# Key gathers and softmax steps of the last four groups of a two-layer graph attention network, done in layer 1's sums' stage instead of its table stage

## The chip, the cores and the metric

The kernel runs on one core of one Trainium2 chip. The metric is the device time of one launch in microseconds. The core has five engines that work side by side, each in the order of its own instructions: PE (TensorE: products and transposes, which write to PSUM), DVE (VectorE), ACT (ScalarE), POOL (GpSimd, which here issues the indirect DMAs, the gathers) and SP (SyncE, which issues most other DMAs).

## What is computed

A graph of 3125 nodes with 53125 edges, sorted by their target `dst`, runs through two layers of relational attention with 3 relations, first with 4 heads and then with 1. The result is added to the input and normalized per row.

```
def rgat_conv(x, W, q, k, b, src, dst, etype, heads, out_ch, n_nodes):
    xr = jnp.einsum('nd,rdf->rnf', x, W)
    oi = xr[etype, dst]
    oj = xr[etype, src]
    qi = oi @ q
    kj = oj @ k
    alpha = jax.nn.leaky_relu(qi + kj, NEG_SLOPE)
    m = jax.ops.segment_max(alpha, dst, num_segments=n_nodes)
    e = jnp.exp(alpha - m[dst])
    z = jax.ops.segment_sum(e, dst, num_segments=n_nodes)
    a = e / (z[dst] + EPS)
    msg = (a[:, :, None] * oj.reshape(-1, heads, out_ch)).reshape(-1, heads * out_ch)
    out = jax.ops.segment_sum(msg, dst, num_segments=n_nodes)
    return out + b

h = elu(rgat_conv(x, W1, q1, k1, b1, ..., 4, 192, n))
out = layernorm(x + rgat_conv(h, W2, q2, k2, b2, ..., 1, 768, n))
```

## The kernel before

Nodes stand in 25 blocks of up to 128 rows. Edges, too, are handled in 25 groups: group b holds the edges of the targets of one block, in 17 slots of 128 edges (14 in group 0), so 14 + 24 x 17 = 422 slots in all. One gather reads, for one slot, one row for each of its 128 edges.

After a preparation (edges in order, per-node scores, weights split into a high and a low part) there are three stages.

**The table stage (`phase1`)** multiplies the blocks 1 to 24 with `W1` for each relation and half: 24 x 6 = 144 products groups (`d_group`, L698, 18 matmuls each), whose results ACT copies (`d_row`, L713) and SP stores in the table `ftab1` (L715). In the same stage the softmax of every edge group of layer 1 is worked out. Its code is a loop over a tick `n`: in each tick the events listed for it come first, and then one products group. For edge group b the events are, with the tick relative to 6b:

- `a_loads`, `a_loads2` (-10, -9): SP loads of the group's edges. `a_index`, `a_index2`, `a_next`, `a_next2` (-6 to -4): a transpose on PE (L541), the indices on DVE, and the start of the next group, each a short exchange of PE and DVE.
- `a_gathers` (-5): the 17 key gathers on POOL (L462, tile `kt`, from the table `kt1` of 4 scores per row), into one of three key buffers.
- `a_q`, `a_q2`, `a_q3` (1 to 3): DVE compares the edges with the node numbers (L601, L603), PE picks each edge's query score (17 small matmuls, L613), DVE reduces them to `qe` (L625, L629).
- `a_window` (2): an SP load of the masks for the scan.
- `a_alpha` (4): DVE adds keys and queries (L634, L636); it needs all keys of the group. `a_max` (5): three transposes on PE (L642). `a_scan` (6): a scan forward and one back on DVE (L650, L651), a subtraction (L654) and the exponential on ACT (L655). `a_back` (7): a transpose back on PE (L659). `a_put` (8): a copy to `pall` (L662), where the weights of all groups are kept. Groups below 8 do these five two ticks later.

Each products group also waits, at three of its matmuls, for a key gather of the edge group that stands at the same place in the order:

```
if n % 6 == 0:
    tc.add_manual_dep(m.ins, gathered[g, (3 * k + n // 6) * slots(g) // 18].name, behind,
                      reason="an even load")
```

In the last 24 ticks ACT also loads layer 2's split weights into the places of `W1` that are free (`second_weights`, L514).

**Layer 1's sums' stage (`phase2`)** is a loop over `k`, one slot each. POOL gathers the slot's rows of `ftab1` (L462, tiles `share` and `g`, 14 buffers in turn); two steps later than it could read them, DVE writes the slot's selection masks times the softmax weights (`high`, L854), and PE sums the rows by target (`sums`, L876) in two batches per group, after 9 and after 17 slots. Each group's sums then go through `e_y` to `e_s2` (DVE, ACT and a transpose on PE, L928) and are multiplied with `W2` (`d_part`, L953, spread over the next group's slots), copied by ACT (L961) and stored by SP in the table of layer 2 (L967). POOL's queue holds the key gathers of the stage before ahead of the first row gather; the last third of the weights of `W2` is loaded by ACT behind the first group's exponential.

**Layer 2's sums' stage (`phase3`)** gathers rows of layer 2's table (tile `G`), works out layer 2's softmax and sums (L1147), and normalizes and stores the result.

The order in each stage is written by hand (the dictionary `ev` of ticks); the compiler does not reorder it. PSUM and SBUF buffers are taken in turn from pools, so a writer waits for the last reader of its buffer.

Of the kernel before, what the change touches and what calls it, by code (L numbers as in the profile page):

```python
# [8 lines left out]
F32 = mybir.dt.float32  # L9
# [4 lines left out]
AF = mybir.ActivationFunctionType  # L14
ALU = mybir.AluOpType
# [5 lines left out]
P = 128  # L21
NEG_SLOPE = 0.2
# [15 lines left out]
SL = 17  # L38
# [10 lines left out]
ROUNDS = ((0, 7, 15), (1, 8, 16), (2, 9, 14), (3, 11), (4, 12), (5, 13), (6, 10))  # L49

BATCHES = ((0, 1, 2), (3, 4, 5, 6))


@with_exitstack
def kernel(
# [19 lines left out]
    nc = tc.nc  # L75
    N, D = x.shape
    R = layers[0]["W"].shape[0]
    E = src.shape[0]
    NB = (N + P - 1) // P
# [4 lines left out]
    H1 = l1["H"]  # L84
# [9 lines left out]
    V, S, G, T = nc.vector, nc.scalar, nc.gpsimd, nc.tensor  # L94
# [6 lines left out]
    ed_d = dram.tile([4, LL], F32, name="ed_d")  # L101
# [3 lines left out]
    kt1 = dram.tile([NP * R, 4], F32, name="kt1")  # L105
# [4 lines left out]
    ident = keep.tile([P, P], F32, name="fident")  # L110
    make_identity(nc, ident)
    row = keep.tile([P, P], F32, name="frow")
# [22 lines left out]
    dl = keep.tile([P, NB, SL + 1], F32, name="fdl")  # L135
    rel = keep.tile([P, NB, SL], F32, name="rel")
    pall = keep.tile([P, NB, SL, H1], F32, name="pall")
# [303 lines left out]
    def base(b):  # L441

        return SLF + (b - 1) * SL if b else 0

    def slots(b):
        return SL if b else SLF

    def slot(k):

        return divmod(k - SLF + SL, SL) if k >= SLF else (0, k)  # L450
# [4 lines left out]
    regs = {}  # L455

    def gather_rows(to, tab, b, j):

        i = ridx[:, b]
        if b in first_rows:  # L460
            i = rfirst[:, first_rows[b]]
        return G.indirect_dma_start(out=to, out_offset=None, in_=tab, in_offset=_index(i[:, j:j + 1]),  # L462
                                    bounds_check=NP * R - 1, oob_is_err=False)

    def start(b, into):

        if b == 0:
            return 0
        if b not in into:
            into[b] = nc.sync.value_load(starts[0:1, 0, b:b + 1], min_val=0, max_val=E)  # L470
        return into[b]
# [7 lines left out]
    def at(t, rw, off, ap, s):  # L479

        c = t[rw:rw + 1, bass.ds(s + (FRONT + off), 1)]
        return bass.AP(tensor=c.tensor, offset=c.offset, ap=ap)
# [37 lines left out]
    def phase1(pre, work, psum, wH, wL, qq):  # L520
# [96 lines left out]
        def a_q3(b):  # L617
            s = st[b]
            pq = s["pq"]
            nq = H1 * R * 3  # L620
            hs = (SL + 1) // 2
            tq = work.tile([P, SL, H1, R * 3], F32, name="tq", bufs=1)
            for c in range(2):
                n = min(hs, SL - c * hs)
                V.tensor_tensor(tq[:, c * hs:c * hs + n],  # L625
                                pq[:, c, :n * nq].rearrange("p (j h k) -> p j h k", j=n, h=H1),
                                s["oh"][:, c * hs:c * hs + n, None, :].to_broadcast([P, n, H1, R * 3]), op=ALU.mult)
            s["qe"] = work.tile([P, SL, H1], F32, name="qe", bufs=2)
            V.tensor_reduce(s["qe"], tq, AX.X, ALU.add)  # L629

        def a_alpha(b):
# [56 lines left out]
        def d_group(n, b, r, c):  # L688

            g, k = divmod(n, 6)  # L690
            po = psum.tile([P, 512], F32, name="po", bufs=2)
            xT = xt[b]
            n = 0
            for t in range(DT):
                i = r * DT + t
                sl = slice(c * HALF, (c + 1) * HALF)
                for s, w in ((0, wH), (0, wL), (1, wH)):
                    m = T.matmul(po[:, :HALF], xT[:, s, t, :], w[:, i, sl], start=(n == 0), stop=(n == 3 * DT - 1))  # L698
                    if n % 6 == 0:
                        tc.add_manual_dep(m.ins, gathered[g, (3 * k + n // 6) * slots(g) // 18].name, behind,  # L700
                                          reason="an even load")
                    n += 1
            st["po", b, r, c] = po

# [67 lines left out]


        GB = NB - 4
        groups = [(b, r, c) for b in range(1, GB) for r in range(R) for c in range(2)]
        groups += [(b, r, c) for r in range(R) for b in range(GB, NB) for c in range(2)]
        ev = {}

        chain = ((-6, a_index), (-6, a_index2), (-5, a_gathers), (-5, a_next), (-4, a_next2))
        for b in range(1, NB):  # L780
            for d, f in chain:
                ev.setdefault(6 * b + d + (b == 1), []).append((f, b))
        steps = ((-10, a_loads), (-9, a_loads2), (1, a_q), (2, a_q2),
                 (2, a_window), (3, a_q3), (4, a_alpha), (5, a_max), (6, a_scan), (7, a_back), (8, a_put))
        for b in reversed(range(NB)):
            for d, f in steps:

                d += 2 * (d >= 4 and b < 8) + (b == 2 and d == -10)
                if 6 * b + d >= 0:
                    ev.setdefault(6 * b + d, []).append((f, b))  # L790
        ev[6 * NB - 10].append((lambda b: a_last(), 0))
        for b in range(2, GB + 1):
            for d, f, o in ((-8, d_turn, 0), (-7, d_split, 0), (-7, x_next, 1)):
# [32 lines left out]
    def phase2(work, psum, wH, wL):  # L826
# [9 lines left out]
        st = {}  # L836
        blk = {}
        order = range(NB)

        def in_turn(k):  # L840

# [3 lines left out]
        def gather(k):  # L845
            gather_rows(gs[k % NG], tab1, *in_turn(k))

        def high(k):

            b, j = in_turn(k)  # L850
            lo, hi = WINDOW[j][0] * 32, WINDOW[j][-1] * 32 + 32
            sel = work.tile([P, H1, 64], F32, name="selp", bufs=12)
            for h in range(H1):
                V.tensor_scalar(sel[:, h, :hi - lo], row[:, lo:hi], dl[:, b, j:j + 1], pall[:, b, j, h:h + 1],  # L854
                                op0=ALU.is_equal, op1=ALU.mult)
            st[b, j] = sel, gs[k % NG]

# [116 lines left out]
        def when(k, f, *a):  # L974
            ev.setdefault(k, []).append((f, a))
# [5 lines left out]
        for i, b in enumerate(order):  # L981
            e = SLF + i * SL + LAG
            if i > 0:
                for d, f in ((0, e_y), (1, e_x), (2, e_h), (3, e_t), (4, e_s), (4, e_s2)):
                    when(e + d, f, b)
            e += 6
            for m in range(6 * R):
                rc = divmod(m // 3, 2)
                k = e + m * SL // (6 * R) if i else first + 5 + m * (SL + 3) // (6 * R)
                when(k, d_part, b, *rc, m % 3)  # L990
                if m % 3 == 2:
                    when(k + 1, d_row, b, *rc)
            when(e + 2 + SL, d_q, b)
        for k in range(max(ev) + 1):
            if k < NK:
                gather(k)
            if k in (19, 20, 23, 26, 28):
                next(last_w2, None)
            if 0 <= k - LAG < NK:
                sums(k - LAG)  # L1000
            if k == first:
                e_first(order[0])
            if 0 <= k - LAG + 2 < NK:
                high(k - LAG + 2)
            for f, a in ev.get(k, []):
                f(*a)
            if k == NK + LAG:
                for b in range(len(xbs)):
                    x_load3(b)
# [882 lines left out]
```

## Time and profile before

| what | value |
|---|---|
| time, median of 3 runs | 2060.18 us (2058.1 to 2061.2) |
| the profiled execution | 2060.05 us, span 2058.3 us |
| mean granted TensorE clock | 0.915 |
| first key gather, first products group | 120.2 us, 123.0 us |
| last key gather | 692.6 us |
| first row gather of layer 1's sums | 693.9 us |
| first row gather of layer 2's sums | 1475.5 us |
| PE busy | 1761.5 us (86%) |
| POOL busy | 1327.4 us (64%) |
| DVE busy | 1185.0 us (58%) |

Times within the execution count from the first instruction. PE's busy time is that of pipelined matmuls, so a busy PE is not PE at its peak. In a line of the timeline, the bracket at the end is the engine's idle time before that instruction and what ended it; "issue" there means that nothing the profile shows was waited for.

### The profile page before, as it was taken

The page shows a single profiled execution, that of the slowest core. Times are in us where ns is not written, and L with a number is a line of the kernel's source. Part 1 is how long each engine was busy: PE and PEld are TensorE (multiplying, and loading weights), DVE is VectorE, ACT ScalarE, POOL GpSimd, SP SyncE. Part 2 cuts the span into 40 slices and gives each one's busy share as a digit, 9 for nine tenths or more (in the row PEclk, how much of TensorE's full clock was granted, in tenths as well). Part 3 has the DMA queues.
Part 4 walks back from the last instruction along what each step waited for, and adds up shares of the span by engine and source line. Part 5 has one row for each costly group of instructions (what it writes and reads, how often), then busy time and mean ns, then how long its engine had stood idle before and what let it go on. Part 6 is the DMA issues. An engine that isn't in the chain of part 4 may idle for free.

```text
span 2058.3 us, 41812 instructions
## 1 busy us (share of the span) xinstructions
PE 1761.5 (86%) x15027; PEld 1482.8 (72%) x15027; DVE 1185.0 (58%) x4163; ACT 374.1 (18%) x659; POOL 1327.4 (64%) x1326
## 2 busy tenths in 40 slices
PE   6989998999999579999999999999666766776775
PEld 5979998899899368988898888888523433433433
DVE  6545554555454456776677667666356556556654
ACT  5421211222111011111111111111102112112111
POOL 4257777777777745556555655564277777777773
PEclk9999999999999889999999999999877777787787
DMA  7655554555547687778777877876699999999993
GB/s 194 192 140 167 176 189 139 172 160 180 176 153 233 216 311 252 258 264 286 250 264 271 279 261 257 280 267 206 223 313 329 343 339 330 339 328 320 320 328 133
DMA packets 156844, 506.31 MB, mean 246 GB/s; under 512 B 43875, under 2 KB 57069, under 8 KB 156628
## 3 DMA queue, kind: packets, MB, share of 16 engines
q0 software_dynamic: 81904, 331.52, 48.2%
q1 hardware_dynamic: 62926, 156.02, 21.8%
q10 hardware_dynamic: 11798, 16.00, 2.3%
q8 instruction: 122, 2.00, 0.4%
q14 instruction: 94, 0.77, 0.1%
HBM read 412.55 MB, written 95.69 MB: 247 GB/s over the span
## 4 chain that ended last, share of the span: by engine, by line
PE 55%; issue 15%; POOL 14%; DMA 10%; DVE 5%; ACT 1%; POOLq 0%; ACTq 0%; DVEq 0%; SPq 0%
PE po L953 23%; PE acc L876 11%; POOL kt L462 11%; PE acc L1147 10%; PE po L698 4%; DMA G<-ftab,ridx 4%; POOL G L462 3%; DMA kt<-kt,ridx 2%; DMA wL<-w_d 2%; PE bank L285 1%; PE pt L263 1%; PE po L395 1%; PE pt L928 1%; DVE F L1107 1%; PE bc L1054 1%
## 5 line engine op out<-in xcount | busy, mean ns | idle before, releaser
L953 PE MATMUL po<-wH,hT 128*128 128x386 f32 (+1 forms) x1800 | 486.7, 345 | 8.5 <-DMA wH<-w_d 5.9
L462 POOL DMA_INDIRECT kt<-kt,ridx x374 | 395.5, 1057 | 114.0 <-issue 110.9
L698 PE MATMUL po<-wH,xT 128*128 128x384 f32 x1584 | 440.6, 348 | 9.7 <-ACT share L713 4.4
L462 POOL DMA_INDIRECT G<-ftab,ridx x374 | 374.2, 1001 | 114.0 <-issue 91.2
L854 DVE TENSOR_SCALAR selp<-frow,fdl,pall 128x32 f32<-128x32 f32 (+1 forms) x1688 | 381.1, 322 | 0.0
L953 PEld LDWEIGHTS po<-wH,hT 128*128 128x128 f32 x1800 | 331.7, 190 | 24.4 <-issue 21.0
L462 POOL DMA_INDIRECT share<-ftab,ridx x239 | 238.4, 997 | 169.8 <-PE acc L876 125.6
L953 PE MATMUL po<-wL,hT 128*128 128x386 f32 (+1 forms) x900 | 306.7, 341 | 4.8 <-DMA wL<-w_d 4.8
L698 PEld LDWEIGHTS po<-wH,xT 128*128 128x128 f32 x1584 | 294.7, 192 | 15.4 <-ACT share L713 6.2
L1147 PE MATMUL acc<-G,selp 128*32 128x386 f32 x2388 | 290.0, 582 | 2.9 <-DVE selp L1133 1.5
L698 PE MATMUL po<-wL,xT 128*128 128x384 f32 x792 | 270.3, 341 | 0.0
L1147 PEld LDWEIGHTS acc<-G,selp 128*32 128x32 f32 x2388 | 178.3, 128 | 77.3 <-issue 45.9
L462 POOL DMA_INDIRECT g<-ftab,ridx x135 | 135.7, 1005 | 108.3 <-PE acc L876 83.0
L876 PE MATMUL acc<-share,selp 128*32 128x193 f32 x3208 | 185.3, 330 | 2.7 <-DMA share<-ftab,rfirst 1.3
L961 ACT COPY r<-po 128x386 f32<-128x386 f32 (+1 forms) x150 | 72.3, 482 | 592.9 <-PE po L953 581.6
L953 PEld LDWEIGHTS po<-wL,hT 128*128 128x128 f32 x900 | 171.3, 190 | 5.2 <-DMA wL<-w_d 5.2
L1060 DVE TENSOR_SCALAR sT<-bc,cols 128x512 bf16<-128x512 f32 (+1 forms) x125 | 83.4, 667 | 150.6 <-PE bc L1054 147.9
L876 PEld LDWEIGHTS acc<-share,selp 128*32 128x32 f32 x3208 | 125.7, 111 | 44.0 <-issue 7.7
L698 PEld LDWEIGHTS po<-wL,xT 128*128 128x128 f32 x792 | 151.7, 191 | 0.0
L1054 PE MATMUL bc<-d,one 1*128 1x512 bf16 (+1 forms) x125 | 48.5, 388 | 85.2 <-DVE sT L1060 82.1
L713 ACT COPY share<-po 128x384 f32<-128x384 f32 x144 | 67.8, 477 | 275.2 <-PE po L698 268.2
L876 PE MATMUL acc<-g,selp 128*32 128x193 f32 x1768 | 115.0, 328 | 1.6 <-DMA g<-ftab,rfirst 1.2
(262 smaller groups left out, 1911.5 us busy)
## 6 DMA issues: line engine op xcount, KB each, us to landing
ftab<-share SPq DMA_DIRECT2D x75, 386.0 KB
ftab<-r SPq DMA_DIRECT2D x75, 386.0 KB
share<-in_L_gnn_W_dram SPq DMA_DIRECT2D x36, 384.0 KB
w_d<-w2hl SPq DMA_DIRECT2D x18, 768.0 KB
sT<-dr_d SPq DMA_DIRECT2D x25, 544.0 KB
share<-in_x_dram SPq DMA_DIRECT2D x27, 384.0 KB
xb_d<-share SPq DMA_DIRECT2D x25, 384.0 KB
xr<-in_x_dram SPq DMA_DIRECT2D x21, 384.0 KB
```

Of the source, the lines that this page charges most:

```text
L263: T.transpose(pt[:, f, c * P:(c + 1) * P], a[:, (2 * i + f) * P:(2 * i + f + 1) * P], ident)
L285: T.matmul(to, a[:, 2 * i + f, :], t[:, f, :w], start=(n == 0), stop=(n == 2 * DT - 1))
L462: return G.indirect_dma_start(out=to, out_offset=None, in_=tab, in_offset=_index(i[:, j:j + 1]), bounds_check=NP * R - 1, oob_is_err=False)
L698: m = T.matmul(po[:, :HALF], xT[:, s, t, :], w[:, i, sl], start=(n == 0), stop=(n == 3 * DT - 1))
L713: S.copy(to, po[:, :HALF].rearrange("p (h f) -> p h f", h=2))
L854: V.tensor_scalar(sel[:, h, :hi - lo], row[:, lo:hi], dl[:, b, j:j + 1], pall[:, b, j, h:h + 1], op0=ALU.is_equal, op1=ALU.mult)
L876: T.matmul(acc[32 * t:32 * t + 32, h // 2, c], sel[:, h, 32 * (t - WINDOW[i][0]):][:, :32], g[:, h * CW:(h + 1) * CW], start=(i == u[0] an ...
L953: T.matmul(po[:, :wd], hT[:, k, t, :], w[:, r * DT + t, sl], start=(t == 0 and n == 0), stop=(t == DT - 1 and n == 2))
L961: S.copy(o[:, c * HW:c * HW + wd], po[:, :wd])
L1054: T.matmul(bc[:, :n], one, s["d"][:, 4 * i * P:4 * i * P + n], start=True, stop=True)
L1060: V.tensor_scalar(s["sT"][:, 4 * i * P:4 * i * P + n], bc[:, :n], cols[:, b:b + 1], None, op0=ALU.is_equal)
L1147: T.matmul(acc[32 * t:32 * t + 32, c, :HW], st[b, j][:, 32 * (t - WINDOW[j][0]):][:, :32], gs[:, (base(b) + j) % NG, c * HW:(c + 1) * HW], ...
```

## The change

The edge groups 21 to 24 (`LATE = 4`) no longer have their keys gathered and their softmax finished in the table stage. Their query scores (`a_q` to `a_q3`) stay there, written to `pall`, which later takes the weights in the same place. Their 68 key gathers go into the loop of layer 1's sums, four at a time (`KEYS = 4`) behind the fourteenth row gather of each of groups 2 to 18, into two new key buffers. Once a group's 17 keys are issued, its mask load, alpha, transposes, scan, exponential, transpose back and copy follow, as `l_load` to `l_put`, 5 to 11 slots behind the sums of group 8, 12, 16 and 20. They use the buffers `y`, `ey` and `pt` of that stage's other steps.

In the table stage, the gathers and softmax steps of the other 21 groups (354 slots) are spread over all 144 ticks: group b stands at tick `turn[b] = base(b) * 144 // 354`, where `base(b)` is its first slot, so one group every 6.9 ticks instead of every 6. All of them now do the last five steps two ticks later. `a_index` to `a_next2` keep their ticks of 6b. The products' waits are for the gather at the same share of 354. The selection masks of layer 1's sums get 8 narrow and 7 wide buffers instead of 12 wide ones.

```diff
+LATE = 4
+KEYS = 4
...
-            s["qe"] = work.tile([P, SL, H1], F32, name="qe", bufs=2)
+            s["qe"] = work.tile([P, SL, H1], F32, name="qe", bufs=2) if b < NB - LATE else pall[:, b]
...
-                        tc.add_manual_dep(m.ins, gathered[g, (3 * k + n // 6) * slots(g) // 18].name, behind,
-                                          reason="an even load")
+                        tc.add_manual_dep(m.ins, gathered[slot((18 * g + 3 * k + n // 6) * NE // (3 * len(groups)))].name,
+                                          behind, reason="an even load")
...
+        NE = base(NB - LATE)
...
+        turn = [base(b) * len(groups) // NE for b in range(NB - LATE)]
         for b in range(1, NB):
             for d, f in chain:
-                ev.setdefault(6 * b + d + (b == 1), []).append((f, b))
+                if f is not a_gathers:
+                    ev.setdefault(6 * b + d + (b == 1), []).append((f, b))
+                elif b < NB - LATE:
+                    ev.setdefault(max(turn[b] + d, 6 * b + d + (b == 1)), []).append((f, b))
         steps = ((-10, a_loads), (-9, a_loads2), (1, a_q), (2, a_q2),
                  (2, a_window), (3, a_q3), (4, a_alpha), (5, a_max), (6, a_scan), (7, a_back), (8, a_put))
+        taken = [n + 2 for n in turn]
+        for b in range(NB - LATE, NB):
+            n = 6 * b + 2
+            while min(abs(n - t) for t in taken) < 2:
+                n += 1
+            taken.append(n)
+            turn.append(n - 2)
         for b in reversed(range(NB)):
             for d, f in steps:
-                d += 2 * (d >= 4 and b < 8) + (b == 2 and d == -10)
-                if 6 * b + d >= 0:
-                    ev.setdefault(6 * b + d, []).append((f, b))
+                if b >= NB - LATE and (d >= 4 or f is a_window):
+                    continue
+                if d == -10:
+                    n = 6 * b + d + (b == 2)
+                elif d == -9:
+                    n = turn[b] - (9 if b < 12 else 4)
+                else:
+                    n = turn[b] + d + 2 * (d >= 4)
+                if n >= 0:
+                    ev.setdefault(n, []).append((f, b))
...
+        kts = [work.tile([P, SL, H1], F32, name=f"kt{i}", bufs=1) for i in range(2)]
+        al = work.tile([P, SL + 2, H1], F32, name="al", bufs=1)
...
+        keys = [(b, j) for b in range(NB - LATE, NB) for j in range(SL)]
+        late = {}
+        def key(b, j):
+            gather_rows(kts[b % 2][:, j, :], kt1, b, j)
+        def l_load(b):
+            t = work.tile([P, D], F32, name="y", bufs=1)[:H1 * SL]
+            late["f"], late["e"] = t[:, :3 * P + 1], t[:, 3 * P + 1:4 * P + 1]
+            nc.sync.dma_start(late["f"], at(ed_d, 3, -P - 1, [[P, SL], [0, H1], [1, 3 * P + 1]], start(b, regs)))
+        def l_alpha(b):
+            kt = kts[b % 2]
+            V.tensor_add(kt, kt, pall[:, b])
+            V.scalar_tensor_tensor(al[:, 1:SL + 1, :], kt, NEG_SLOPE, kt, op0=ALU.mult, op1=ALU.max)
+        def l_max(b):
+            late["pa"] = psum.tile([P, 2, 512], F32, name="pt", bufs=1)[:, 0, :]
+            for c in range(3):
+                T.transpose(late["pa"][:H1 * SL, c * P:(c + 1) * P],
+                            al.rearrange("p j h -> p (j h)")[:, c * H1:(c + SL) * H1], ident)
+        def l_scan(b):
...
+            V.tensor_tensor_scan(F, f[:, 0:3 * P], pa[:H1 * SL, :3 * P], -3e38, op0=ALU.add, op1=ALU.max)
+            V.tensor_tensor_scan(B[:, ::-1], f[:, P + 1:3 * P + 1][:, ::-1], F[:, P:3 * P][:, ::-1], -3e38,
+                                 op0=ALU.add, op1=ALU.max)
+            V.tensor_sub(e, pa[:H1 * SL, P:2 * P], B[:, :P])
+            S.activation(e, e, AF.Exp)
+        def l_back(b):
+            T.transpose(late["pa"][:, 3 * P:3 * P + H1 * SL], late["e"], ident[:H1 * SL, :H1 * SL])
+        def l_put(b):
+            V.tensor_copy(pall[:, b].rearrange("p j h -> p (j h)"), late["pa"][:, 3 * P:3 * P + H1 * SL])
...
-            sel = work.tile([P, H1, 64], F32, name="selp", bufs=12)
+            sel = work.tile([P, H1, hi - lo], F32, name=f"selp{hi - lo}", bufs=8 if hi - lo == 32 else 7)
...
+        at_key = {base(2 + i // KEYS) + 13: keys[i // KEYS * KEYS:i // KEYS * KEYS + KEYS]
+                  for i in range(0, len(keys), KEYS)}
+        for i in range(LATE):
+            e = base(2 + (SL * (i + 1) - 1) // KEYS + 2) + LAG
+            for d, f in ((5, l_load), (6, l_alpha), (7, l_max), (8, l_scan), (10, l_back), (11, l_put)):
+                when(e + d, f, NB - LATE + i)
         for k in range(max(ev) + 1):
             if k < NK:
                 gather(k)
+            for i in at_key.get(k, ()):
+                key(*i)
```

More of the change, by code (lines that the diff above doesn't have):

```diff
@@ L838, in phase2 @@
         order = range(NB)
+        kts = [work.tile([P, SL, H1], F32, name=f"kt{i}", bufs=1) for i in range(2)]
+        for t in kts:
+            V.memset(t, 0.0)
+        al = work.tile([P, SL + 2, H1], F32, name="al", bufs=1)
+        V.memset(al, 0.0)
+        keys = [(b, j) for b in range(NB - LATE, NB) for j in range(SL)]
[16 more added lines that the diff above has]
+        def l_scan(b):
+            pa, f, e = late["pa"], late["f"], late["e"]
+            t = work.tile([P, D], F32, name="ey", bufs=1)[:H1 * SL]
+            F, B = t[:, :3 * P], t[:, 3 * P:5 * P]
+            V.tensor_tensor_scan(F, f[:, 0:3 * P], pa[:H1 * SL, :3 * P], -3e38, op0=ALU.add, op1=ALU.max)
[7 more added lines that the diff above has]
+            V.tensor_copy(pall[:, b].rearrange("p j h -> p (j h)"), late["pa"][:, 3 * P:3 * P + H1 * SL])
         def in_turn(k):
@@ L851, in high @@
             lo, hi = WINDOW[j][0] * 32, WINDOW[j][-1] * 32 + 32
-            sel = work.tile([P, H1, 64], F32, name="selp", bufs=12)
+            sel = work.tile([P, H1, hi - lo], F32, name=f"selp{hi - lo}", bufs=8 if hi - lo == 32 else 7)
             for h in range(H1):
-                V.tensor_scalar(sel[:, h, :hi - lo], row[:, lo:hi], dl[:, b, j:j + 1], pall[:, b, j, h:h + 1],
+                V.tensor_scalar(sel[:, h, :], row[:, lo:hi], dl[:, b, j:j + 1], pall[:, b, j, h:h + 1],
                                 op0=ALU.is_equal, op1=ALU.mult)
```

## The prediction

> **What bounds the kernel now.** I read the page first, then the windows, then the timelines where one stage hands over to the next.
>
> From the page: the chain's shares and the two gather groups.
>
> ```profile
> PE 55%; issue 15%; POOL 14%; DMA 10%; DVE 5%; ACT 1%; POOLq 0%; ACTq 0%; DVEq 0%; SPq 0%
> L462 POOL DMA_INDIRECT kt<-kt,ridx x374 | 395.5, 1057 | 114.0 <-issue 110.9
> L462 POOL DMA_INDIRECT share<-ftab,ridx x239 | 238.4, 997 | 169.8 <-PE acc L876 125.6
> ```
>
> The key gathers (kt) are followed by idle time that nothing but POOL's own issue ends; the row gathers of layer 1's sums (share) wait for PE to release buffers. POOL is the bound in the table stage and has slack in the sums' stage.
>
> The windows of L698, the table's products, 18 to a group; columns: busy time and count, granted clock, DMA share, GB/s.
>
> ```profile
> 173.30:240.60 67.30, 60.85 (x325) 1.00 0.60 189
> 450.60:493.60 43.00, 40.34 (x216) 1.00 0.56 180
> 173.30:676.40 503.10, 445.47 (x2358) 0.99 0.56 179
> ```
>
> The whole stretch is 131 groups in 503.1 us, 3.840 us each. Two stretches without a wait for keys go faster: 43.0/12 = 3.583 and 67.3/18 = 3.739.
>
> The handover, POOL's and then PE's timeline (start, duration, what; in brackets the idle time before it and what ended it).
>
> ```profile
> 691.32 1.00 POOL L462 DMA_INDIRECT kt<-kt,ridx  x1 [0.30 <-issue]
> 692.62 1.00 POOL L462 DMA_INDIRECT kt<-kt,ridx  x1 [0.30 <-issue]
> 693.92 1.00 POOL L462 DMA_INDIRECT share<-ftab,rfirst  x1 [0.30 <-issue]
> ```
>
> ```profile
> 680.56 0.59 PE L613 MATMUL pq<-q,sT 128*128 128x36 bf16 x17
> 695.47 0.82 PE L642 MATMUL pa<-fident,al 128*68 128x128 f32 x3 [14.32 <-DVE al L636]
> ```
>
> POOL goes without a pause from the last key to the first table row, and PE stands idle 14.3 us before it. So 693.92, the first row gather, is set by POOL: 422 gathers from 120.17, (693.92-120.17)/422 = 1.36 us each.
>
> The sums' stage: POOL's timeline in one group, and the chain's pieces from the first row gather on.
>
> ```profile
> 886.22 0.99 POOL L462 DMA_INDIRECT share<-ftab,ridx  x1 [0.30 <-issue]
> 893.99 0.99 POOL L462 DMA_INDIRECT share<-ftab,ridx  x1 [6.78 <-PE acc L876]
> ```
>
> ```profile
> 721.93 42.87 DMA wL<-w_d
> 768.10 5.64 PE po L953 x30
> 1472.02 2.36 DMA ftab<-r
> ```
>
> Once per group, behind its fourteenth gather, POOL idles 6.78 us. PE's pieces follow each other without gaps there (a group takes 29.65 us: its piece of 30 products starts at 798.11, 827.75, 857.36 and so on), so this stage is PE's.
>
> **The change, part by part.**
>
> *Fewer keys ahead of the rows.* 68 of the 422 key gathers leave the table stage. The 354 left need 354 x 1.36 = 481 us from 120.17, so POOL would be done at 602, even somewhat later where it waits for a key buffer. It stops being the bound, and late is then PE: 144 groups of products, then the last table store.
>
> *PE's pace.* The products' own waits are now spread as 354 gathers over 144 groups, 2.46 x 1.36 = 3.3 us a group, under any pace above; these waits go. The waits of `a_max` for alpha (14.8 us on PE in the table stage, behind the last key of each group) go too, since a group's alpha now stands eleven ticks behind the start of its gathers, some 40 us, for 17 x 1.36 = 23 us of gathers. What is left is the pace without key waits, 3.583 to 3.739. The difference of these two is `a_back`, PE's transpose back: early, the scan falls in the tick where DVE also serves `a_next2`, and PE waits for it. The new ticks are 6.85 groups apart instead of 6, so the scan drifts through all six places of the cycle, four of them with other DVE work that PE hands over and two without; and 20 sets of softmax steps replace 24. I take 3.67. From 173.3, 131 x 3.67 = 480.8 brings the last group to 654.1 and its end (3.4 us) to 657.5; with the two paces, 646.1 and 666.5.
>
> *From PE's end to the first row gather.* The nearest row is the other handover: layer 2's last product ends at 1471.4, its store takes 2.36 us (above), and the first gather of the next stage starts at 1475.54, so 4.1 us. I take 5, as weight loads may still be under way. First row gather: 662.5 instead of 693.92, a gain of 31.4 us. Bounds: 651 and 672, gains of 43 and 22.
>
> *From there to the steady groups.* Today it takes 768.10-693.92 = 74.2 us, of which 42.87 are the last four weight loads behind row gathers. ACT issues them behind the first group's exponential, so they move along: nothing gained, nothing lost. `second_weights`, `x_load` and the rest keep their ticks.
>
> *Keys in the sums' stage.* Four gathers stand behind the fourteenth gather of groups 2 to 18, where POOL idles 6.78 us, 0.30 of it issue. Four of them take 4 x 1.30 = 5.2 (the pitch of the rows above), by the mean of kt's group 4 x 1.36 = 5.4. They fit with 1 us to spare, and I cost them at nothing. Without that cover they would cost 5.4 us in each of 17 groups, less the 2 us that 21 gathers of 1.30 leave in 29.65.
>
> *Softmax steps in the sums' stage.* Four times: on PE three transposes and one back, 0.49 and 0.28 us in the table stage's rows (L642, L659), so 4 x 0.77 = 3.1 on a full PE. On DVE two additions, two scans, a subtraction and a copy, 0.23+0.23+0.94+0.69+0.28+0.22 = 2.6 us, which DVE's idle stretch of 4.98 us before 933.15 (it waits there for ACT) hides, and the sums read their masks later still. On SP the window's load is queued behind table stores already issued. The exponential (0.31 us) stands on ACT ahead of copies that PE waits for with two banks. If all were exposed it is 4 x (0.77+2.6+0.3) = 15 us; I take 3.5, near PE's part, since everything else has idle time.
>
> [...]
>
> [...]
>
> *Mask tiles, `qe` in `pall`.* The mask buffers (8 narrow, 7 wide for 12) let DVE run as far ahead as before, and the reduction only changes its target: 0.
>
> **Sum.** The profiled execution took 2060.05 us, span 2058.3; the median is 2060.18, so no scaling. The last stage is POOL's from 1475.54 and shifts as a whole. 2060.05 - 31.4 + 3.5 = 2032.
>
> **Rivals.** *The scan behind `a_q` (slower).* The new ticks put the next group's `a_q` (L601 and L603, 1.01+0.30 = 1.3 us on DVE) into the tick of the scan and ahead of it, and PE's `a_back` waits one tick later. Where it is exposed in all 20 groups, the last product ends at 666.5+26 = 692.5, the first row gather comes at 697.5, and the time is 2060.05+3.6+3.5 = 2067. It decides from a pace of 3.88 on, 0.14 above the slower clean stretch. Against: `a_q` waits for no work of PE's tick, so in half the places DVE has done it early.
>
> *Keys overrun their gap (slower).* If a key takes 2.6 us beside rows, 21 gathers take 17 x 1.3 + 10.4 = 32.5 us, 2.9 over the group, 17 times: 2032+49 = 2081. It turns against the change from about 2.3 us a key on. Against: 1057 ns in its group.
>
> *The start does not follow (smaller gain).* The loads of layer 2's first two thirds (eight of 1152 KB) now stand closer to the first rows. If half of them is left at 662, 4.6 MB at the 390 GB/s of 665 to 682 take 12 us: 2044.
>
> **How the numbers follow.** The forecast as worked out 0.80, the start not following 0.10, `a_q` 0.05, keys 0.03, gains and losses that cancel 0.02. Low: first row at 650.2, 2060.05-43.7+3 = 2019, so 2020. High: pace 3.739 (-22.4) with half of the exposed softmax steps and a few waits for `a_q` (+12) = 2050. 0.2% is 4 us, about what this kernel's measurement tells apart: faster 0.90, same 0.02, slower 0.08.
>
> **What would show it.** The first row gather at 651 to 672 behind an idle POOL, released by the last table store; kt x354 ended by about 610; PE's 14.3 us wait gone; L698 at about 3.67 us a group, with what it still waits for named ACT or DVE, not DMA kt; the 6.78 us gap filled by four kt rows and PE's groups still at 29.65, four of them 0.8 longer. It is wrong if PE's last product ends after 680, or if groups 2 to 18 of the sums' stage take over 30 us.

## The result and the profile after

The changed kernel takes 2031.26 us in the median of four runs (2027.43 to 2032.23), the kernel before 2059.57 us beside it (2058.1 to 2061.2). The ratio is 0.9852 with a 95% interval of 0.9834 to 0.9869: 28 us saved, where 28 were forecast. The profiled execution took 2031.11 us with a span of 2029.3 us, 29.0 below the span before.

The page of the changed kernel first: the chain's shares by engine, then the groups of key gathers and row gathers (busy time and mean ns, then idle time ahead of them and what ended most of it).

```profile
PE 73%; DMA 9%; DVE 7%; issue 5%; POOL 3%; ACT 1%; SPq 0%; POOLq 0%; ACTq 0%; DVEq 0%
L466 POOL DMA_INDIRECT kt<-kt,ridx x374 | 400.6, 1071 | 114.7 <-issue 109.3
L466 POOL DMA_INDIRECT share<-ftab,ridx x239 | 239.0, 1000 | 119.9 <-PE acc L942 73.9
```

POOL's share of the chain fell from 14% to 3% and that of issue, which was mostly POOL's, from 15% to 5%; PE's rose from 55% to 73%. The number of key gathers is that of before, and their cost is nearly so (1071 ns for 1057). What differs is their place, and the row gathers idle 49.9 us less (119.9 for 169.8), since keys stand in their gaps.

Next the stretch of the table's products, L702 now, from the same group 12 on as before; columns: window, length, PE's busy time and count, weight loads, granted clock, DMA share, GB/s.

```profile
177.60:655.80 478.20, 438.98 (x2359) 409.79 (x2360) 1.00 0.57 185
```

131 groups take 478.2 us, 3.650 each (3.840 before). Now the handover on POOL's timeline, with the idle time ahead of an instruction in brackets, and PE's last product.

```profile
607.48 1.00 POOL L466 DMA_INDIRECT kt<-kt,ridx  x1 [0.30 <-issue]
608.78 1.00 POOL L466 DMA_INDIRECT kt<-kt,ridx  x1 [0.30 <-issue]
663.92 1.00 POOL L466 DMA_INDIRECT share<-ftab,rfirst  x1 [54.14 <-ACT e L659]
665.22 1.00 POOL L466 DMA_INDIRECT share<-ftab,rfirst  x1 [0.31 <-DVE selp L920]
```

```profile
658.77 0.34 PE L702 MATMUL po<-wH,w2hl 128*128 128x384 f32 x1
```

POOL's last key starts at 608.78 (692.62 before), and then POOL stands idle for 54.14 us. The first row gather comes at 663.92, 30.0 us earlier than before and 4.81 us after the end of the last product (659.11). The line names the exponential of group 20 as releaser, which ended at 662.92; the last table store landed at 662.88. The two are too close to tell apart here.

In the sums' stage, POOL's timeline in one group, around its fourteenth row gather:

```profile
855.69 0.99 POOL L466 DMA_INDIRECT share<-ftab,ridx  x1 [0.31 <-issue]
856.99 1.00 POOL L466 DMA_INDIRECT kt<-kt,ridx  x1 [0.30 <-issue]
858.29 1.00 POOL L466 DMA_INDIRECT kt<-kt,ridx  x1 [0.30 <-issue]
859.59 1.00 POOL L466 DMA_INDIRECT kt<-kt,ridx  x1 [0.30 <-issue]
860.89 1.00 POOL L466 DMA_INDIRECT kt<-kt,ridx  x1 [0.30 <-issue]
863.48 0.99 POOL L466 DMA_INDIRECT share<-ftab,ridx  x1 [1.58 <-PE acc L942]
```

The 6.78 us gap of before now holds four keys, and POOL still waits 1.58 us for PE behind them. The chain's pieces in a group with a softmax (start, length, what):

```profile
909.54 5.46 PE po L1019 x30
...
921.09 0.33 PE pt L887 x3
...
928.84 0.06 PE pt L901
...
939.64 5.46 PE po L1019 x30
...
969.28 5.46 PE po L1019 x30
```

The group that starts at 909.54 is the one with softmax steps: 30.10 us, of which the three transposes hold 0.33 and the one back 0.06. The next takes 29.64 us, as before. From the first row gather to the first group at this pace it is 127.0 us (663.92 to 790.94) and was 127.6 (693.92 to 821.53). From there to the first gather of layer 2's sums, 1446.57, it is 655.6 us and was 654.0. That gather starts 28.97 us earlier than before, and the rest moves with it as a whole.

### The profile page after: what moved, and what is told of

The parts are those of the page before. It is cut to its first block, busy times and chain, and to the rows that moved or that the text cites. A ratio compares the mean times of both kernels' runs of the same rounds, so it can differ in the third digit from the quotient of the medians.

```text
span 2029.3 us, 41799 instructions
## 1 busy us (share of the span) xinstructions
PE 1753.6 (86%) x15027; PEld 1479.9 (73%) x15027; DVE 1183.6 (58%) x4166; ACT 373.6 (18%) x659; POOL 1333.3 (66%) x1326
## 4 chain that ended last, share of the span: by engine, by line
PE 73%; DMA 9%; DVE 7%; issue 5%; POOL 3%; ACT 1%; SPq 0%; POOLq 0%; ACTq 0%; DVEq 0%
PE po L1019 23%; PE po L702 20%; PE acc L942 11%; PE acc L1221 10%; DMA G<-ftab,ridx 4%; POOL G L466 3%; DMA wL<-w_d 2%; PE bank L289 2%; PE pt L267 1%; DMA sT<-dr_d 1%; PE po L399 1%; DMA share<-in_L_gnn_W_dram 1%; PE pt L994 1%; DVE F L1181 1%; PE px L679 1%
## 5 line engine op out<-in xcount | busy, mean ns | idle before, releaser
L466 POOL DMA_INDIRECT kt<-kt,ridx x374 | 400.6, 1071 | 114.7 <-issue 109.3
L702 PE MATMUL po<-wH,xT 128*128 128x384 f32 x1584 | 435.1, 346 | 6.5 <-ACT share L717 2.8
L920 DVE TENSOR_SCALAR selp<-frow,fdl,pall 128x32 f32<-128x32 f32 (+1 forms) x1688 | 382.5, 325 | 0.0
L466 POOL DMA_INDIRECT share<-ftab,ridx x239 | 239.0, 1000 | 119.9 <-PE acc L942 73.9
L702 PEld LDWEIGHTS po<-wH,xT 128*128 128x128 f32 x1584 | 291.9, 190 | 10.3 <-ACT share L717 4.7
L702 PE MATMUL po<-wL,xT 128*128 128x384 f32 x792 | 269.1, 340 | 0.0
L702 PEld LDWEIGHTS po<-wL,xT 128*128 128x128 f32 x792 | 150.6, 190 | 0.0
L1128 PE MATMUL bc<-d,one 1*128 1x512 bf16 (+1 forms) x125 | 48.2, 386 | 85.8 <-DVE sT L1134 82.6
L717 ACT COPY share<-po 128x384 f32<-128x384 f32 x144 | 67.9, 477 | 289.8 <-PE po L702 264.1
```

The costliest lines, as they stand in the source:

```text
L717: S.copy(to, po[:, :HALF].rearrange("p (h f) -> p h f", h=2))
L920: V.tensor_scalar(sel[:, h, :], row[:, lo:hi], dl[:, b, j:j + 1], pall[:, b, j, h:h + 1], op0=ALU.is_equal, op1=ALU.mult)
L1128: T.matmul(bc[:, :n], one, s["d"][:, 4 * i * P:4 * i * P + n], start=True, stop=True)
```

## The experiments

Each edit is told against the changed kernel. Each ratio is to the kernel before in the same comparison, on the same chip; there that kernel took 2063.04 us beside `move_only`, `pace_only`, `late1` and `late2`, and 2061.45 us beside the next four. The landmarks are from each kernel's own trace, in us; the last key is that of the table stage, and a dash stands where the value was not worked out.

| kernel | time | ratio to before | last key | first row gather | products, per group | first gather, layer 2 |
|---|---|---|---|---|---|---|
| before | 2059.57 | 1 | 692.6 | 693.9 | 3.840 | 1475.5 |
| the change | 2031.26 | 0.9852 (0.9834 to 0.9869) | 608.8 | 663.9 | 3.650 | 1446.6 |
| move_only | 2046.59 | 0.9922 (0.9905 to 0.9939) | 603.0 | 680.1 | 3.787 | 1463.3 |
| pace_only | 2100.64 | 1.0180 (1.0163 to 1.0197) | 725.8 | 736.6 | 4.21 | 1518.5 |
| late1 | 2051.68 | 0.9945 (0.9929 to 0.9962) | 675.3 | 685.7 | 3.837 | 1466.7 |
| late2 | 2034.24 | 0.9863 (0.9846 to 0.9879) | 657.1 | 668.1 | 3.677 | 1450.5 |
| late1_nowait | 2052.63 | 0.9955 (0.9938 to 0.9971) | 677.2 | 686.3 | – | 1468.8 |
| keys8 | 2053.50 | 0.9963 (0.9950 to 0.9975) | 609.6 | 663.5 | – | 1465.0 |
| keys17 | 2077.43 | 1.0080 (1.0062 to 1.0099) | 608.7 | 661.2 | – | 1492.1 |
| scan_first | 2023.33 | 0.9819 (0.9799 to 0.9840) | 613.1 | 655.6 | 3.602 | 1439.4 |

**Moving alone and pacing alone.** `move_only` moves the four groups and leaves all other ticks, and the products' waits, as they were before:

```diff
-                        tc.add_manual_dep(m.ins, gathered[slot((18 * g + 3 * k + n // 6) * NE // (3 * len(groups)))].name,
-                                          behind, reason="an even load")
+                        at_ = (g, (3 * k + n // 6) * slots(g) // 18) if g < NB - LATE else (NB - LATE - 1, SL - 1)
+                        tc.add_manual_dep(m.ins, gathered[at_].name, behind, reason="an even load")
...
-        turn = [base(b) * len(groups) // NE for b in range(NB - LATE)]
+        turn = [6 * b for b in range(NB - LATE)]
...
-        taken = [n + 2 for n in turn]
-        for b in range(NB - LATE, NB):
-            n = 6 * b + 2
-            while min(abs(n - t) for t in taken) < 2:
-                n += 1
-            taken.append(n)
-            turn.append(n - 2)
+        turn += [6 * b for b in range(NB - LATE, NB)]
...
-                    n = turn[b] - (9 if b < 12 else 4)
+                    n = 6 * b - 9
...
-                    n = turn[b] + d + 2 * (d >= 4)
+                    n = turn[b] + d + 2 * (d >= 4 and b < 8)
```

> The 68 keys and four softmaxes are moved, but the other 21 groups keep their ticks of before (6b, five steps two ticks later only below group 8) and the products their waits of before. Theory (the first row gather comes at the later of POOL's last key and PE's last product): POOL is done at about 602, but PE keeps the old pace, since each group's alpha still waits for its last key; its last product ends at about 678 as before, the first row gather comes at about 683 instead of 694, and the time is about 2050. Rival (the move alone frees the start, the pace does nothing): about 2031 as with the whole change.

`pace_only` moves nothing (`LATE = 0`) and spreads all 422 gathers over the 144 ticks by the new formula:

```diff
-LATE = 4
+LATE = 0
...
-                        tc.add_manual_dep(m.ins, gathered[slot((18 * g + 3 * k + n // 6) * NE // (3 * len(groups)))].name,
+                        tc.add_manual_dep(m.ins, gathered[min(slot((18 * g + 3 * k + n // 6) * NE // (3 * len(groups))), max(gathered))].name,
                                           behind, reason="an even load")
...
-                    n = turn[b] - (9 if b < 12 else 4)
+                    n = max(turn[b] - (9 if b < 12 else 4), 6 * b - 9)
```

> Nothing is moved (LATE = 0): all 25 groups' gathers and softmax steps stand in the table stage, spread over the 144 ticks at the pace of 422 gathers. Theory: POOL still has 422 gathers ahead of the first row, so that comes at about 694 and the time is 2058 to 2062. Rival (PE's waits for keys are what counts): the table stage ends some 15 us earlier, about 2045.

`move_only` saves 16.5 us. Its handover on POOL's timeline, then the window of its products:

```profile
602.99 1.00 POOL L466 DMA_INDIRECT kt<-kt,ridx  x1 [0.31 <-issue]
680.09 1.00 POOL L466 DMA_INDIRECT share<-ftab,rfirst  x1 [76.10 <-issue]
```

```profile
177.00:673.00 496.00, 442.97 (x2360) 0.99 0.56 180
```

POOL has been done for 76 us when PE's last products let the rows start. So moving the keys takes POOL out of the end of the stage, and PE's pace of 496/131 = 3.787 us is then the bound: 13.8 of the 30.0 us at the first row gather. The other 16.2 come with the new ticks, by which PE goes at 3.650. In `move_only`'s stretch PE still waits 12.8 us at the transposes for alpha.

`pace_only` was a miss, 38 us slower than before. The waits of PE up to 740 us (total, times, longest), and those of POOL up to 720:

```profile
PE po L702 <- DMA kt<-kt,ridx: 49.8, 45, 4.5
```

```profile
POOL kt L466 <- DVE lim L561: 28.5, 8, 7.1
```

PE's products wait 45 times for a key gather, and POOL waits up to 7.1 us for the indices of its next keys. Those are computed in ticks of 6b, which go forward only with PE's products. So there is a ring: products behind keys, keys behind indices, indices behind products. With 422 gathers in 144 ticks POOL has no slack to catch up in. POOL's waits for indices are most of the 33.2 us by which its last key comes later than before. That the ring costs the whole 38 us is argued from these waits and not shown: the run without the products' waits, `pace_nowait` below, stands in a comparison that cannot be set beside this one.

**How many groups must move.** `late1` and `late2` set `LATE = 1` and `LATE = 2`, with the `max` above.

> One group is moved instead of four (17 keys), the pace that of 405 gathers. Theory: POOL ends at 120 + 405 x 1.36 = 671, some 7 us after PE would let the rows begin, so the first row gather comes at about 672 and the time is about 2038. Rival (the gain goes with the number of moved gathers, 29 us for 68): 7 us, about 2053.

> Two groups are moved (34 keys), the pace that of 388 gathers. Theory: POOL ends at 120 + 388 x 1.36 = 648, before PE's last product at about 659, so the first row gather comes at about 664 as with four groups, and with two softmaxes fewer in the sums' stage the time is 2030 to 2032. Rival (the gain goes with the number of moved gathers): 14 us, about 2045.

By the times, two groups give what four give: 2034.24 us, 28.8 saved. One group gives 11.4, between the two expectations and nearer to the rival's. The handover on POOL's timeline, `late1` and then `late2`:

```profile
675.27 0.99 POOL L466 DMA_INDIRECT kt<-kt,ridx  x1 [0.30 <-issue]
685.66 0.99 POOL L466 DMA_INDIRECT share<-ftab,rfirst  x1 [9.40 <-DMA ftab<-share]
```

```profile
657.10 0.99 POOL L466 DMA_INDIRECT kt<-kt,ridx  x1 [0.30 <-issue]
668.13 1.00 POOL L466 DMA_INDIRECT share<-ftab,rfirst  x1 [10.04 <-DMA ftab<-share]
```

In both POOL waits for the table's last store. But in `late1` PE comes late to its last product, 681.97 (664.34 in `late2`), at 3.837 us a group. PE could be held by the products' own waits for keys, 22.0 us in this trace, or by something else that hangs on the keys. `late1_nowait` takes these waits out:

```diff
-                        tc.add_manual_dep(m.ins, gathered[slot((18 * g + 3 * k + n // 6) * NE // (3 * len(groups)))].name,
-                                          behind, reason="an even load")
```

> As late1 (17 keys moved), but the products' waits for key gathers (the even load) are left out; each group's alpha still waits for its keys. In late1 the products waited 22 us for keys, because 405 keys over 144 ticks are asked for before POOL, held up by the indices at ticks of 6b, has them. Theory (the products' waits made late1 lose 10 us against the first sum): POOL's last key comes at about 671, the first row gather at about 673, and the time is about 20 us below the kernel before. Rival (POOL is late for another reason, an index or a buffer): no change, some 11 us below before.

Nothing changes: 2052.63 us, and the first row gather 0.7 us later. Its waits of PE up to 690:

```profile
PE pa L646 <- DVE al L640: 22.6, 12, 2.7
```

The same 22 us now stand at the transposes of alpha, which need all 17 keys of a group. On PE's queue the last groups' transposes stand ahead of the last products. So PE doesn't end its products much before POOL's last key, wherever it waits: the first row gather comes 10.4 us behind that key in `late1` and 9.1 here. With 405 gathers ahead POOL still sets the end: in `late1` its one long wait for DVE, 15.2 us, is at the start of the stage, and it goes on at its own pace from there. With 388 it nearly stops doing so; this is the wait for keys that PE has left in `late2`, up to 664:

```profile
PE po L702 <- DMA kt<-kt,ridx: 5.0, 8, 1.7
```

With four groups moved that row is gone, and the first row gather of the trace comes 4.2 us earlier than in `late2`.

**How many keys fit behind the fourteenth gather.** `keys8` and `keys17` issue 8 or 17 at a time, in fewer groups.

> The same with 8 keys at a time, in groups 2 to 10. Theory: 25 gathers take 32.5 us of POOL against 29.65, 2.9 us over in each of eight groups, of which some 8 us of lead are used up first: about 15 us longer than the whole change. Rival (hidden wherever they stand): as with the whole change.

> The 68 keys of the sums' stage stand 17 at a time behind the fourteenth gather of groups 2 to 5, not 4 at a time behind that of groups 2 to 18. Theory (only POOL's idle gap of 6.8 us hides them): four groups in a row have 34 gathers, 44 us of POOL against PE's 29.65; less the start, where POOL idles anyway, and about 8 us of lead, it costs 30 to 35 us, and the gain is gone: about as long as the kernel before. Rival (key gathers are hidden behind PE wherever they stand): as with the whole change.

Against the change, by the ratios, they lose 23 us and 47 us (2061.45 x 0.9852 = 2030.9 for the change), more than expected both times; in the traces, the way from the first row gather to layer 2's first gather is 801.5 and 830.9 us instead of 782.65. POOL's timeline in one group of `keys17`, where the keys end, the rows go on and the next keys begin:

```profile
832.87 1.00 POOL L466 DMA_INDIRECT kt<-kt,ridx  x1 [0.30 <-issue]
834.17 1.00 POOL L466 DMA_INDIRECT g<-ftab,ridx  x1 [0.30 <-DMA kt<-kt,ridx]
...
855.04 1.00 POOL L466 DMA_INDIRECT g<-ftab,ridx  x1 [0.30 <-PE pt L887]
856.35 1.00 POOL L466 DMA_INDIRECT kt<-kt,ridx  x1 [0.30 <-DVE q L1031]
```

POOL makes no pause. This batch of keys began at 811.83 and the next at 856.35: 44.5 us for 34 gathers, 1.31 each, where PE would need 29.65. In `keys8`, too, POOL makes no pause over 0.5 us from 760 to 1031. The rival of keys that overrun their gap is thus a real mechanism. At 1.30 us each, 22 gathers fit into 29.65 us: four keys a group make 21, eight make 25.

It is not the whole loss, though. The load of the scan's masks, which the change hides, comes too late in these two kernels. DVE's waits for it between 700 and 1440 us, in the change and then in `keys8`, and PE's waits behind it in `keys8`:

```profile
DVE ey L894 <- DMA y<-ed_d: 5.0, 3, 2.1
```

```profile
DVE ey L894 <- DMA y<-ed_d: 22.2, 4, 7.5
PE pt L901 <- ACT y L898: 9.4, 3, 3.7
```

PE has no such wait in the change; in `keys17` the two rows are 27.0 and 13.4 us. So 9.4 of the 18.9 us that `keys8` loses in its trace, and 13.4 of the 48.2 of `keys17`, stand at the softmax steps. What is left, 9.5 and 34.8 us, is what the other waits cost, the keys' overrun among them. How far the late mask load is itself a consequence of POOL's lag, no run shows.

**The scan behind `a_q`.** In each tick the loop over groups takes the later group first, so `a_q` of the next group stands on DVE ahead of the scan. `scan_first` turns this round:

```diff
-        for b in reversed(range(NB)):
+        for b in range(NB):
             for d, f in steps:
```

> The whole change, but within a tick the steps of the lower group come first, so that DVE works on the scan ahead of the next group's a_q. Theory (the pace of 3.65 us a products group holds waits of PE's transpose back for a scan behind a_q, some 8 us on PE): PE's table stage ends 5 to 10 us earlier, and the whole time falls by as much against the whole change. Rival (the waits only move to a_q2, which then waits for a_q): no change.

In the changed kernel, the waits of PE from 123 to 665 and one such scan on the timeline of all engines:

```profile
PE pa L663 <- ACT e L659: 5.5, 6, 1.9
```

```profile
207.89 0.78 DVE L605 TENSOR_SCALAR sT<-sT,cols 128x2176 bf16<-128x2176 bf16 x1
208.58 0.32 DVE L607 TENSOR_TENSOR oh<-rel,rel 128x153 f32<-128x153 f32 x1
208.81 0.94 DVE L654 TENSOR_TENSOR_SCAN share<-w,pa 68x384 f32<-68x384 f32 x1
...
211.19 0.28 PE L663 MATMUL pa<-fident,e 68*128 68x68 f32 x1 [0.51 <-ACT e L659]
```

The two instructions of `a_q` end just as the scan begins, and PE's transpose back waits for what follows from the scan. PE waits for it in a second way, too: ACT keeps its order, and its copies of the products (L717) stand behind the exponential. Each of PE's four waits for these copies in the stretch (2.8 us in all) comes 1.0 to 1.5 us after the start of an exponential for which ACT had waited 6.8 us or more, as here:

```profile
210.83 0.31 ACT L659 ACTIVATE e<-e 68x128 f32<-68x128 f32 x1 [7.34 <-DVE e L658]
212.28 0.44 PE L702 MATMUL po<-wH,xT 128*128 128x384 f32 x1 [0.82 <-ACT share L717]
```

With the order turned, the handover and the window of the products:

```profile
613.10 1.00 POOL L466 DMA_INDIRECT kt<-kt,ridx  x1 [0.30 <-issue]
655.58 1.00 POOL L466 DMA_INDIRECT share<-ftab,rfirst  x1 [41.48 <-issue]
```

```profile
176.00:647.90 471.90, 438.74 (x2358) 409.47 (x2359) 1.00 0.58 188
```

471.9/131 = 3.602 us a group, the first row gather 8.3 us earlier, and PE's waits for this exponential 2.5 us instead of 5.5. PE's waits for the copies are gone; all its idle time in the stretch falls from 5.4 us to 0.9. Of the 8.3 us, 6.3 come in the stretch and 1.6 ahead of it. At 2023.33 us (2019.44 to 2028.07) it lies below both kernels. Its ratio's interval overlaps that of the change at the edge (0.9834 to 0.9840), so the times alone do not settle that it is the faster one; the step itself is seen in the traces.

**Without the products' waits, and earlier weights.** Four more kernels were compared: the change once more, the change and `pace_only` without the products' waits, and `scan_first` with the last third of layer 2's weights loaded at earlier steps of the sums' loop (`k in (6, 7, 8, 9, 28)` for `(19, 20, 23, 26, 28)`).

> The whole change once more, on the chip of the runs beside it, as their yardstick: 28 to 29 us below the kernel before.

> The whole change without the products' waits for key gathers (the even load). Theory (with 354 gathers POOL is ahead of every one of these waits): within 3 us of the whole change, and PE's pace in the table stage stays at 3.65 us a group. Rival (the waits still hold the products back): 5 to 10 us faster.

> As pace_only (nothing moved, 25 groups spread over the ticks), but without the products' waits for key gathers. In pace_only these waited 49 us. Theory (a ring: products ask for keys at an even pace, the keys need indices that PE's ticks of 6b bring, so both slow down; without the waits only POOL's 422 gathers are left as bound): POOL's last key at about 695, the first row gather at about 700, the time within 10 us of the kernel before. Rival (the later softmax ticks themselves are slow): 2090 or more.

> scan_first, and the last third of layer 2's weights is loaded by ACT ahead of the first group's exponential instead of behind it (the loop steps 6 to 9 instead of 19 to 26). Theory (DMA moves 310 to 395 GB/s in the 70 us behind the first row gather, so the order of the loads changes little): within 4 us of scan_first, since the first rows come later by what the weights come earlier. Rival (PE's 9.6 us wait for these weights is lost time): 8 to 10 us below scan_first.

These give no answer. In this comparison the kernel before itself took 2671.48 us, and the four 2671.6, 2671.37, 2608.71 and 2676.85 us. Three of PE's longer waits in the changed kernel's trace there:

```profile
PE po L702 <- issue: 68.1, 83, 6.4
PE acc L942 <- issue: 40.5, 138, 1.6
PE pq L617 <- issue: 20.7, 17, 11.0
```

Here PE stands idle between instructions for nothing that the profile names; the mean granted clock is 0.852 instead of 0.918. The preparation takes the same 123 us as elsewhere, the products from group 12 on 5.05 us a group, and layer 1's sums' stage 1064.6 us instead of 782.65. The change saves nothing there: 1.0014 (0.9988 to 1.0040). In its trace POOL is done 75 us ahead of the first row gather, so it is not POOL that ends the table stage; whether it was in the kernel before, there, is not known, as no trace of that one was taken. Why `pace_nowait` is 2.5% faster than before there (0.9751, 0.9727 to 0.9776) is open. So it stays open whether the products' waits still cost the change anything, and whether earlier weights help it; PE waited 9.6 us for `wL` in the changed kernel's trace.

## Why the prediction was right

**POOL no longer ends the table stage.** The forecast was a last key by about 610 and a first row gather behind an idle POOL: 608.8, and 54 us of idle time. `move_only` shows this part alone, and `late1` where it ends: with one group moved, POOL still decides.

**PE's pace.** 3.67 us a group was taken from two stretches without a wait for keys, and 3.650 was measured. The reason given for the difference of those two stretches was only half right. In the slower one, 173.3 to 240.6 of the trace before, PE does not wait at the transpose back at all. Its idle time there, 1.9 us, is three waits for ACT's copies, which stand behind the late exponential; that is 0.105 of the 0.156 us a group. The rest is more work of PE. So the scan was the cause, but by another way, and that 3.67 lay so near was in part luck. The last group started at 655.8 (forecast 654.1) and the first row gather at 663.9 (forecast 662.5). The last group's 1.7 us lie ahead of the stretch: group 12 begins 4.3 us later than before, and the pace gives 2.6 back. The 4.3 us are the longer wait at 137.87 (2.72 us for 1.71 in the trace before), the slower clock behind it (11 products at 0.32 instead of 0.175, 1.6 us) and one more wait of 1.61 us for the exponential. That `a_max`'s wait for alpha would go is right too: 29.1 us of waits at the transposes of L642 in the trace before are no longer among PE's waits. `move_only`, which keeps the old ticks, still has 12.8.

**From PE's end to the first gather**: 5 us taken, 4.81 measured; in `scan_first` 4.33, in `move_only` 3.97. Whether the changed kernel's store or its exponential was last can't be told from its trace. In the four traces whose line names the store (`late1`, `late2`, `late1_nowait`, `pace_only`) it is 3.69 to 3.79, so the store alone may need some 1 us less than the change took. Against that, in `scan_first` the exponential ended 1.6 us ahead of the gather, at 654.02, and the interval is only 0.5 us shorter. It stays open.

**Keys cost nothing in the sums' stage.** A spare of 1 us was forecast, and 1.58 - 0.30 = 1.28 us was left. `keys8` and `keys17` show that more keys than the gap holds do cost, though a part of their loss stands at the softmax steps. One sign of being wrong, a group over 30 us, did come up to the letter: the four groups with softmax steps take 30.1 us each. But the prediction had itself put 0.8 us more on these four, and the others keep 29.64.

**The softmax steps are the term that was mis-sized**: 3.5 us forecast, 1.6 measured (655.6 less 654.0 for the steady groups), 0.4 for each of the four. They were costed by the durations of the table stage's rows, 0.49 and 0.28. But a matmul's duration in the profile overlaps with its neighbours' (the table's products last 0.34 us and start 0.175 apart), and what counted on a full PE was the time until the next one started: 0.33 and 0.06 in the chain above, 4 x 0.39 = 1.56. DVE's, ACT's and SP's parts were hidden, as forecast: from 740 to 1440 us the trace lists no wait of PE. Even a scan that waited 2.12 us for its mask load did not reach the chain:

```profile
924.62 0.95 DVE L894 TENSOR_TENSOR_SCAN ey<-y,pt 68x384 f32<-68x384 f32 x1 [2.12 <-DMA y<-ed_d]
```

The sum comes out with two small errors against each other, which is luck: 1.4 us less at the first row gather and 2.5 more behind it (1.9 in the groups, 0.6 in the start).

**Contention and the clock.** The 1688 masks of the sums' stage (L920) took 382.5 us in all beside 68 more gathers, and 381.1 before, so no contention with gathers is seen in them. Nor in the trace before: there, 16 masks took 3.59 us with POOL idle (918.40), 0.224 each, and 24 took 5.30 us mostly beside gathers (922.86), 0.221 each.

The granted clock fell in the table stage. PE's timeline at the longest wait of the table stage:

```profile
137.87 0.58 PE L617 MATMUL pq<-q,sT 128*128 128x36 bf16 x17 [2.72 <-DVE own L572]
138.29 0.64 PE L702 MATMUL po<-wH,xT 128*128 128x384 f32 x1
138.72 0.52 PE L702 MATMUL po<-wL,xT 128*128 128x384 f32 x1
139.04 0.84 PE L702 MATMUL po<-wH,xT 128*128 128x384 f32 x2
```

Behind 2.72 us of idle time the products start 0.32 us apart for some 3.6 us, at a granted clock of 0.51 (138.3 to 141.8), and then 0.175 apart again, at 1.00. Behind 1.61 us (166.50) they went on at 0.175. `move_only` has a wait of 2.73 us (135.10), too, behind which they kept 0.175 for 5 us, over one more wait of 1.36 us (139.13), and stood 0.32 apart from 141.0 on. In the trace before, seven products stood 0.32 apart behind a wait of 2.23 us (332.30), at a granted clock of 0.50 (332.8 to 335.2). So a lower clock followed some of these waits and not others, and their length alone does not decide. From group 12 to the last group no wait of PE in the changed kernel was over 0.82 us, and the granted clock of the stretch was 1.00.

**The rivals.** The scan behind `a_q` did come, at part strength. It was priced at 26 us if exposed in all 20 groups; turning the order round brings 8.3 us at the handover. It did not decide, since the pace with it was 3.650 and not the 3.88 from which it would. Keys did not overrun their gap at four a group; with eight they do. The start of layer 1's sums did follow: 127.0 us to the first steady group, 127.6 before, and the last load of `wL` took 41.30 us instead of 42.87. The 390 GB/s in that rival were read too high: the trace before has 269 over 665 to 682.

## What to carry to other kernels

Before work is moved off an engine that ends a stage, look for the second engine's end and its pace without the first one's waits: here two moved groups were enough, and the other two bought nothing that the times could tell. A gap on an in-order queue is worth the whole instructions that fit into it at their issue pitch (here four gathers at 1.30 us in 6.78 us, not eight), and what hangs on the moved work, here the load of the scan's masks, needs its own slack (DVE waited 22.2 us for it in `keys8`, 5.0 in the change). Price short instructions on a full engine by the distance to the next start, not by their own duration (here 0.39 us a set, not 0.77), and look at the order inside a tick: a further 8 us at the handover came from swapping which group goes first.

## What the runs showed of the hardware

Most indirect gathers occupied POOL for 1.30 us from start to start, 1.00 busy and 0.30 to the next, for 128 rows of 16 bytes (keys) and for 128 rows of the table alike (medians of 0.997 and 0.998 us busy in the changed kernel's trace). Waits moved rather than vanished: with the products' waits for keys taken out, 22.6 us stood at the transposes of alpha (`late1_nowait`) where 22.0 had stood at the products (`late1`).

A late exponential on ACT held up PE twice over, at the transpose that needs it (5.5 us in six waits of the changed kernel's table stage) and, 1.0 to 1.5 us later, at products whose copies stood behind it in ACT's order (2.8 us in four). Behind a wait of 2.72 us TensorE ran at little more than half its pace for 3.6 us (products 0.32 us apart, not 0.175), at a granted clock of 0.51; behind one of 2.73 us in `move_only` it kept its pace for 5 us. And one and the same program took 2671.6 us instead of 2031.3 where PE's instructions came late without a releaser in the profile, while POOL's gathers kept their 1.30 us.
